# A four-layer graph network: one flat list of steps for layer 3, and its first distances moved into layer 2

## The chip, the cores and the metric

The kernel runs on one core of one Trainium2 chip. The metric is the device time of one execution in microseconds (us). Before the change it is 673.0 us, the median of three runs (672.6 to 673.97).

A core has engines that run side by side, each with its own queue of instructions, which it takes strictly in the written order: TensorE (PE; PEld is its loading of weights), VectorE (DVE), ScalarE (ACT), GpSimd (POOL) and SyncE (SP, which here issues the loads). An instruction that waits holds up everything behind it on its engine.

## The reference, cut to what matters

Four layers share one weighted adjacency matrix of 3327 x 3327 and node features of width 64. Each has the form

```python
h = jnp.maximum(_layernorm(x, axis=-1), 0.0)
x = x + layer(h, adj, ...)
```

Layer 0 is a pair of gated graph convolutions, layer 1 a sum over neighbours in hyperbolic space, layer 2 a sum over the last 100 neighbours of each node with halving weights. Layer 3 is attention in hyperbolic space:

```python
x_tan = _logmap0(x, C)
left = x_tan @ att_W[:D] + att_b
right = x_tan @ att_W[D:]
adj_att = jax.nn.sigmoid(left + right.T) * adj
x_local = _logmap(x[:, None, :], x[None, :, :], C)
support_t = jnp.einsum('ij,ijd->id', adj_att, x_local)
return _proj(_expmap(x, support_t, C), C)
```

So for every pair of nodes layer 3 needs a distance (a dot product and a function of it), an attention weight and their product, and then sums over one index.

## The kernel before

The nodes are padded to 26 blocks of 128. Two blocks make one of 13 columns, and the columns form two groups: `GROUPS[0]` (the code's `gs_`) has columns 0 to 5, `GROUPS[1]` (`gf`) columns 6 to 12. The adjacency is streamed from memory in tiles of up to 896 KB. `Stream` issues the loads on SP in the order of use, into a number of slots (four in layer 3), and loads the next tile when `stream.done()` frees one.

**Layer 2.** `count` makes counts of neighbours on PE into one of two PSUM pairs, ACT or DVE turn them into weights (L1676, L1678), and `weigh` sums with these weights on PE (L1690, six matmuls each). `flush` writes out the sums that are still to do. The group `gf` is finished first; its normalization, node terms and first attention terms (`nodes3(gf, ...)`, `early3`) run woven into the counts of `gs_`.

**Layer 3** uses that distances are symmetric. Its work is cut into 13 phases (`PHASES`), each with up to seven column pairs and two halves `b`. Phases 0 to 3 concern columns of `gf` alone, phases 4 to 9 one column of `gs_` each against all of `gf`, phases 10 to 12 columns of `gs_` alone. The steps of a phase, with their engines:

- `distances` (L1223): matmuls into a PSUM pair, in two pieces `i` of four and three columns. `gelus` (L1233, ACT) reads the pair into the tile `sq`; `square` (L1243, ACT) squares it.
- `tanh_d` (L1256) and `tanh_t` (L1280), ACT: attention terms, in the direct and in the turned arrangement; tiles `dir` and `tr`.
- `attention_d` and `attention_t` (L1293, DVE): times the adjacency tile.
- `turned` (L1323, PE): the distances transposed into the PSUM pair 1, in two pieces. `factors_t` (L1330, DVE) multiplies them into `tr`; `factors_d` (L1311, DVE) multiplies `sq` into `dir`.
- `gather_d`, `gather_t` and `singles` (L1339, PE): the sums, in PSUM banks.

The order of all this is written out. `ORDER3` holds three lists: one for phase 0, one that is repeated for phases 1 to 11, one for phase 12. An entry such as `factors_t.1.0.0` means the step of the phase before (late by 1). Three more chains are woven in as generators: `nodes3(gs_, ...)` (node terms of the first group, about 37 pieces), `bound` (a test of the smallest norm, L1584 to L1589) and `finish_f` (the end of `gf`: L1419 to L1447). `weave.tick()` at an entry `tick` moves what is running one piece further; `WAITS3` gives how many ticks pass between pieces. `distances` of phase 4 first completes `nodes3` and runs `bound`.

`nodes3(gs_, ...)` is a serial chain. The sums of layer 2 are evicted to `m_t` (L638 ACT, L640 DVE), turned by PE (L537) and added to `xn` (L997, DVE); mean, centred value `xc`, variance (L1001 to L1024, DVE and ACT, with two loads of ACT tables at L1016 and L989); `h` and `xd` (L1026, L1028, DVE); `xd` turned by PE (L526) and copied to `xs` (L1048); the attention products (L1057, PE); packed rows `rows_i` and `rows_j` (L1116 to L1121); `leftb` (L1139 to L1144). Phases 4 and later need it, phases 0 to 3 don't.

`finish()` (from L1495) ends the kernel: it closes both sums, applies the last maps, and stores. A further block of code for small norms stands behind a branch on `within`, which `values_load` reads into a register, and isn't run with these inputs.

Of the kernel before, what the change touches and what calls it, by code (L numbers as in the profile page):

```python
# [8 lines left out]
F32 = mybir.dt.float32  # L9
# [10 lines left out]
P = 128  # L20
# [132 lines left out]
BETWEEN = len(PHASES)  # L153
PHASES += [Phase((c,), COLS[1]) for c in COLS[0]]
WITHIN = len(PHASES)
# [40 lines left out]
def order3(text):  # L196
    r = []
    for line in text.split("\n"):
        for name, *args in (w.split(".") for w in line.split()):
            r.append((name, *map(int, args)))  # L200
    return r


EARLY3 = ("d0", "t0")
ORDER3 = [
    order3(t)
    for t in (
        """
        distances.0.0.0 gelus.0.0.0 distances.0.0.1 tanh_t.0.1.0 tick.0 tanh_t.0.1.1 tick.0 tick.0
        tick.1 gelus.0.0.1 square.0.0 distances.0.1.0 gelus.0.1.0 tick.0 distances.0.1.1 tick.0  # L210
        tick.0 tick.0 gelus.0.1.1 tick.0 tick.0 square.0.1 tick.1 tick.0 tick.1 tick.1 tick.0
        tick.1 tick.1 distances.-1.0.0 turned.0.0.0 tick.0 tick.0 tanh_d.0.1 tick.0 gelus.-1.0.0
        """,
        """
        factors_t.1.0.0 tick.0 distances.0.0.1 tick.1 turned.1.0.1 attention_d.1.0 tick.1
        tanh_t.0.0.0 singles.2.1 gelus.0.0.1 distances.0.1.0 tick.1 square.0.0 factors_t.1.0.1
        tick.0 turned.1.1.0 factors_d.1.0 gelus.0.1.0 tanh_d.0.0 tick.1 tick.0 gather_t.1.0.0
        attention_t.1.1 end.2 tick.0 distances.0.1.1 gelus.0.1.1 square.0.1 tanh_t.0.0.1 tick.1
        factors_t.1.1.0 singles.1.0 turned.1.1.1 attention_d.1.1 distances.-1.0.0 factors_t.1.1.1
        tanh_d.0.1 tanh_t.0.1.0 tick.0 factors_d.1.1 tick.0 turned.0.0.0 tick.0 attention_t.0.0  # L220
        tanh_t.0.1.1 gather_t.1.1.1 tick.0 gelus.-1.0.0 gather_t.1.1.0 gather_d.1.0 gather_t.1.0.1
        gather_d.1.1
        """,
        """
        distances.0.0.1 factors_t.1.0.0 tick.1 turned.1.0.1 tanh_t.0.0.0 attention_d.1.0 tick.1
        singles.2.1 gelus.0.0.1 distances.0.1.0 square.0.0 factors_t.1.0.1 gelus.0.1.0
        factors_d.1.0 turned.1.1.0 tanh_d.0.0 tick.1 end.2 attention_t.1.1 factors_t.1.1.0
        distances.0.1.1 singles.1.0 attention_d.1.1 gelus.0.1.1 square.0.1 turned.1.1.1
        tanh_t.0.0.1 tick.1 tanh_t.0.1.0 factors_t.1.1.1 gather_t.1.0.1 factors_d.1.1
        gather_t.1.0.0 tanh_d.0.1 gather_d.1.0 gather_t.1.1.0 turned.0.0.0 attention_t.0.0  # L230
        gather_d.1.1 gather_t.1.1.1 factors_t.0.0.0 tanh_t.0.1.1 turned.0.0.1 tick.1
        attention_d.0.0 singles.1.1 tick.1 factors_t.0.0.1 factors_d.0.0 tick.1 tick.1
        turned.0.1.0 end.1 gather_t.0.0.0 tick.1 attention_t.0.1 factors_t.0.1.0 singles.0.0
        turned.0.1.1 attention_d.0.1 factors_t.0.1.1 tick.1 gather_t.0.1.0 factors_d.0.1
        gather_d.0.0 gather_t.0.1.1 gather_t.0.0.1 gather_d.0.1 tick.1 singles.0.1 end.0 tick.1
        """,
    )
]

WAITS3 = (1, 1, 1, 1, 1, 1, 1, 1, 1, 1, 1, 1, 1, 1, 3, 1, 1, 1, 1, 1, 1, 1, 1, 2, 3, 1, 1, 1, 1, 1)


class Stream:
# [67 lines left out]
def gnn_kernel(ctx: ExitStack, tc: tile.TileContext, t, out):  # L313
    nc = tc.nc
    V, S, G, T = nc.vector, nc.scalar, nc.gpsimd, nc.tensor
# [33 lines left out]
    WIDE = 2 * max(g.w for g in GROUPS)  # L349
# [17 lines left out]
    places, _ = places3()  # L367
# [133 lines left out]
    def pair(i):  # L501

        return ps.tile([P, 1024], F32, name="pair", tag=f"pair{i}")

    def bank(i):
        return ps.tile([P, 512], F32, name="bank", tag=f"bank{i}")
# [639 lines left out]


    def wide3(name, tag):
        pool = n3f if tag in EARLY3 else wk
        return pool.tile([P, WIDE], F32, name=name, tag=tag)  # L1150

    STEPS3 = {}
    made3 = set()

    def step3(f):
        STEPS3[f.__name__] = f
# [34 lines left out]
    @step3  # L1191
    def distances(m, b, i):


        nonlocal x2_
        ph = PHASES[m]
        if m == BETWEEN and x2_ is None:
            weave.until(gen_s)
            for _ in bound():
                pass  # L1200
            x2_ = bank(1)
            V.memset(x2_, 0.0)
        lo, hi = chunk(m, i)
        p = pts[m, b, i] = pair(0)
        g, s = ph.g, ph.s
        for c, ts, first in ph.runs:
            a, e = max(lo, first), min(hi, first + len(ts))
            n = (e - a) * P
            if n <= 0:
                continue  # L1210
            ca = ts[a - first]
            j0 = s.off + b * s.w + (c - s.c0) * P
            for rows in (False, True):
                for k in range(2):
                    rs = slice(k * D, (k + 1) * D)
                    i0 = g.off + k * g.w + (ca - g.c0) * P
                    if rows:
                        l, r = rows_j[rs, j0 : j0 + P], rows_i[rs, i0 : i0 + n]
                    else:
                        l = (xs if k == b else xw)[rs, c * P : (c + 1) * P]  # L1220
                        r = xs[rs, ca * P : ca * P + n]
                    o = k * 512 + (a - lo) * P
                    T.matmul(p[:, o : o + n], lhsT=l, rhs=r, start=not rows, stop=rows)  # L1223
# [117 lines left out]
    @step3  # L1341
    def gather_d(m, b):
        nonlocal pp_
        if (m, b) == (n_all - 1, 1):
            assert (m, "singles", 0) in made3
            pp_ = flat(big(GROUPS[1], "sq"))[:, : 4 * P].rearrange("p (s i c) -> p s i c", s=2, i=2)
            copied_singles(0, ps_)
        a = columns(dirs[m, b], PHASES[m].n)
        for c, ts, first in PHASES[m].runs:
            for p, o, lo, hi in runs(ts, place):  # L1350
                for k in range(2):
                    add(
                        p[k * D : (k + 1) * D, o : o + (hi - lo) * P],
                        xd[:, 2 * c + b, :],
                        a[:, k, (first + lo) * P : (first + hi) * P],
                    )
# [236 lines left out]
        yield  # L1593

    n_all = len(PHASES)
    def have(m):
        return 0 <= m < n_all

    @step3
    def end(m):  # L1600

        nonlocal final
        for d in (sqs, dirs, trs):
            for b in range(2):
                d.pop((m, b))
        if m == WITHIN - 1:
            final = weave.add(finish_f())

    def early3():

        for name, *args in (("tanh_t", 0, 0), ("tanh_t", 0, 1), ("tanh_d", 0)):
            made3.add((0, name, *args))
            yield from STEPS3[name](0, *args)


    with ExitStack() as c2:
# [101 lines left out]
        for n in range(len(work)):  # L1718
# [37 lines left out]
            V.tensor_scalar(onesl, last[:12, :].to_broadcast([12, P]), 9.0, None, op0=OP.is_ge)  # L1756
            gen_n = weave.add(nodes3(gf, m_f))
            weave.add(early3(), 1, gen_n)
        flush(len(work) + LAG, len(todo))
        while weave.running:  # L1760
            weave.tick()
        for name, *args in (("attention_t", 0), ("attention_d", 0)):
            made3.add((0, name, *args))
            STEPS3[name](0, *args)
        x0, x1 = bank(2), bank(3)
        for a in (x0, x1):
            V.memset(a, 0.0)
        m_s = evicted(gs_, acc2[0], b_l2)
    c012.close()
    stream.close(range(SLOTS3, SLOTS2))  # L1770


    turn["banks"] = (1,)
    gen_s = weave.add(nodes3(gs_, m_s), waits=WAITS3)

    with ExitStack() as cf:
        wk = cf.enter_context(right("wkf"))

        ps_, x2_, late_, ds_, pp_ = bank(0), None, None, None, None
        V.memset(ps_, 0.0)

        within = n3.tile([1, 1], I32, name="within")
        final = None
        begin, loop, rest = ORDER3
        orders = [(0, begin)] + [(m, loop) for m in range(1, n_all - 1)] + [(n_all - 1, rest)]
        for m, order in orders:
            for name, late_by, *args in order:  # L1790
                if name == "tick":

                    if late_by or m < BETWEEN:
                        weave.tick()
                elif have(m - late_by) and (m - late_by, name, *args) not in made3:
                    made3.add((m - late_by, name, *args))
                    for _ in STEPS3[name](m - late_by, *args) or ():
                        pass
            if m == WITHIN + 1:
                ok = nc.values_load(within, min_val=0, max_val=1)  # L1800
        weave.until(final)
        finish()
    c3.close()


    with ExitStack() as cg:
        cg.enter_context(tc.If(ok < 1))
        g3 = cg.enter_context(right("g3"))
        sums = g3.tile([P, NB, D + 1], F32, name="sums")

# [366 lines left out]
```

## Time and profile before

| What | Value |
|---|---|
| Median of three runs | 673.0 us |
| The profiled execution's own time | 672.22 us |
| Its span, first to last instruction | 670.4 us |
| Mean granted clock of TensorE | 0.977 |
| PE busy, share of the span | 615.3 us, 92% |
| DVE busy | 456.5 us, 68% |
| ACT busy | 389.3 us, 58% |
| First matmul of layer 3 (L1223) | 416.23 us |
| Last matmul of its main part (`singles` 12.1) | 650.33 us |

Times in the text count from the start of the span. The page has the span in 40 equal slices of 16.8 us, with a digit for the busy share in tenths (9 is 90% or more) and a line `PEclk` for the clock granted to TensorE, in tenths of full speed. A row of the waits reads: waiting line, releasing line, us in total, number of times, longest. A row of the timeline reads: start, us, engine and line, operation, tiles with shapes, number of instructions, and in brackets the idle time before it with its releaser. Matmuls overlap, so the time of a group is best read from its start to the start of the next.

### The profile page before, as it was taken

The numbers are of one execution on the slowest core, as the hardware profiler recorded it, in microseconds if no ns is written. First come the engines' busy times: TensorE is split into PE (matmuls) and PEld (weight loads), VectorE is DVE, ScalarE is ACT, GpSimd is POOL, SyncE is SP. The second block draws the span as 40 slices with busy tenths as digits, with TensorE's granted clock in tenths as the row PEclk, the third lists the DMA queues.
The fourth block names the chain that finished last, engine by engine and source line by source line (L and its number), as shares of the span: only waits on it lengthen the run. The fifth ranks groups of instructions, "written<-read, shape, count | busy, mean of one in ns | idle before, by whom it ended". The sixth has DMA issues, their size and how long they took to land.

```text
span 670.4 us, 13972 instructions
## 1 busy us (share of the span) xinstructions
PE 615.3 (92%) x5968; PEld 341.3 (51%) x5968; DVE 456.5 (68%) x725; ACT 389.3 (58%) x561; POOL 9.3 (1%) x19
## 2 busy tenths in 40 slices
PE   2988999999989999899998999599999999999994
PEld 1442334244333334256665666266666666666781
DVE  3231865444688822678648755679999999999876
ACT  3011300220264403298888688879999999999813
POOL 0000000000000000100000100000000000000000
PEclk9999999999999999999999999589999999999997
DMA  8999999179996999998788993226776666666401
GB/s 335 414 388 421 374 374 351 80 258 421 418 415 228 406 417 415 419 376 318 254 272 294 308 332 118 82 62 188 248 228 221 221 221 221 220 197 221 152 2 56
DMA packets 32534, 183.46 MB, mean 274 GB/s; under 512 B 3696, under 2 KB 4752, under 8 KB 32464
## 3 DMA queue, kind: packets, MB, share of 16 engines
q1 hardware_dynamic: 32112, 181.63, 73.7%
q0 software_dynamic: 352, 0.85, 0.5%
q8 instruction: 49, 0.80, 0.5%
q14 instruction: 21, 0.17, 0.1%
HBM read 180.76 MB, written 0.85 MB: 271 GB/s over the span
## 4 chain that ended last, share of the span: by engine, by line
PE 61%; DVE 18%; DMA 9%; ACT 9%; issue 3%; SPq 0%; ACTq 0%; DVEq 0%
PE bank L651 22%; PE bank L1339 11%; DMA adj<-in_adj 8%; PE pair L1666 7%; PE bank L1690 6%; PE pair L1223 4%; DVE dir L1293 2%; DVE dir L1311 2%; PE pair L752 2%; DVE tr L1330 2%; DVE tr L1293 2%; PE pair L1323 2%; ACT w L1678 2%; ACT tr L1280 1%; DVE edges L379 1%
## 5 line engine op out<-in xcount | busy, mean ns | idle before, releaser
L651 PE MATMUL bank<-adj,m_a 128*64 128x384 f32 (+1 forms) x832 | 154.4, 518 | 8.7 <-DMA adj<-in_adj 6.1
L651 PEld LDWEIGHTS bank<-adj,m_a 128*64 128x64 f32 x832 | 56.9, 137 | 96.2 <-issue 70.9
L1678 ACT ACTIVATE w<-pair,ebias 128x896 uint16<-128x896 f32 (+1 forms) x101 | 93.4, 954 | 17.2 <-PE pair L1666 16.0
L651 PE MATMUL bank<-adj,m_b 128*64 128x384 f32 (+1 forms) x416 | 76.9, 515 | 1.9 <-ACT hm L740 1.4
L379 DVE SCALAR_TENSOR_TENSOR edges<-adj,edges 128x1792 bf16<-128x1792 f32 (+1 forms) x24 | 45.0, 1890 | 32.8 <-DMA adj<-in_adj 32.7
L1280 ACT ACTIVATE tr<-leftb,righth 128x256 f32<-128x256 f32 x156 | 66.3, 495 | 0.1
L1635 DVE TENSOR_SCALAR mask<-adj 128x1792 bf16<-128x1792 f32 (+1 forms) x52 | 52.8, 1035 | 18.8 <-PE pair L1666 18.8
L740 ACT ACTIVATE hm<-bank 64x384 f32<-64x384 f32 (+1 forms) x8 | 4.1, 513 | 94.9 <-DVE mh L739 94.6
L1223 PE MATMUL pair<-xs 64*128 64x512 f32 (+3 forms) x120 | 56.3, 556 | 3.1 <-ACT sq L1233 3.1
L1223 PE MATMUL pair<-xs,xw 64*128 64x512 f32 (+3 forms) x120 | 56.3, 556 | 1.2 <-ACT sq L1233 1.1
L1330 DVE SCALAR_TENSOR_TENSOR tr<-pair,tr 128x1024 f32<-128x1024 f32 (+3 forms) x52 | 49.7, 956 | 9.9 <-PE pair L1323 7.5
L1690 PE MATMUL bank<-w,m_b 128*64 128x384 bf16 (+1 forms) x416 | 56.2, 339 | 0.0
L1233 ACT ACTIVATE sq<-pair 128x1024 f32<-128x1024 f32 (+1 forms) x52 | 47.2, 907 | 13.4 <-PE pair L1223 12.7
L651 PEld LDWEIGHTS bank<-adj,m_b 128*64 128x64 f32 x416 | 28.9, 137 | 46.5 <-issue 41.7
L1311 DVE SCALAR_TENSOR_TENSOR dir<-sq,dir 128x1792 f32<-128x1792 f32 (+2 forms) x27 | 52.5, 1946 | 0.0
L1293 DVE SCALAR_TENSOR_TENSOR dir<-dir,adj 128x1792 f32<-128x1792 f32 x26 | 52.4, 2016 | 0.0
L1256 ACT ACTIVATE dir<-leftb,righth 128x1792 f32<-128x1792 f32 (+6 forms) x38 | 48.5, 1307 | 0.0
L1243 ACT ACTIVATE sq<-sq,hg 128x1792 f32<-128x1792 f32 x26 | 46.5, 1790 | 0.8
L1293 DVE SCALAR_TENSOR_TENSOR tr<-tr,adj 128x1280 f32<-128x1280 f32 (+2 forms) x26 | 45.5, 1751 | 0.0
L1339 PE MATMUL bank<-dir,xd 128*64 128x384 f32 (+3 forms) x264 | 43.7, 461 | 0.0
L1339 PE MATMUL bank<-dir,p2c 128*32 128x256 f32 (+1 forms) x424 | 42.7, 345 | 0.0
L1339 PE MATMUL bank<-tr,xd 128*64 128x128 f32 x624 | 42.0, 277 | 0.0
(312 smaller groups left out, 924.3 us busy)
## 6 DMA issues: line engine op xcount, KB each, us to landing
adj<-in_adj SPq DMA_DIRECT2D x108, 896.0 KB, 6.5
adj<-in_adj SPq DMA_DIRECT2D x92, 768.0 KB, 8.3
adj<-in_adj SPq DMA_DIRECT2D x12, 640.0 KB, 4.1
xn<-in_x SPq DMA_DIRECT2D x3, 192.0 KB, 5.2
out<-w SPq DMA_DIRECT2D x3, 192.0 KB, 2.5
xw<-xs POOLq DMA_DIRECT2D x4, 128.0 KB, 4.0
w_l<-in_w_l SPq DMA_DIRECT2D x1, 460.0 KB, 9.7
xn<-in_x SPq DMA_DIRECT2D x1, 256.0 KB, 6.9
```

What stands on the lines that cost most here:

```text
L379: V.scalar_tensor_tensor(e, a, 0.0, e, op0=OP.not_equal, op1=OP.add)
L651: T.matmul(acc[q][h * D : (h + 1) * D, : hi - lo], lhsT=m[:, k, :], rhs=a[:, h * g.w + lo : h * g.w + hi], start=first, stop=last,)
L1223: T.matmul(p[:, o : o + n], lhsT=l, rhs=r, start=not rows, stop=rows)
L1256: S.activation(columns(dirs[m, b], ph.n)[:, :, first * P : first * P + n], left_of(ph.g)[:, :, o : o + n], AF.Tanh, bias=righth[:, 2 * c + ...
L1280: S.activation(a[:, 8 * u * P : (8 * u + 2 * n) * P].rearrange("p (r x c) -> p x r c", r=2, c=D)[:, 2 * i : 2 * i + 2], left_of(ph.s)[:, : ...
L1293: V.scalar_tensor_tensor(a[:, :w], a[:, :w], 1.0, stream.tile(stream.now), op0=OP.add, op1=OP.mult)
L1311: V.scalar_tensor_tensor(a[:, :, cs], s[:, :, cs], HD, a[:, :, cs], op0=OP.add, op1=OP.mult)
L1330: V.scalar_tensor_tensor(a, p, HD, a, op0=OP.add, op1=OP.mult)
L1339: T.matmul(out, lhsT=lhsT, rhs=rhs, start=False, stop=True, skip_group_check=True)
L1635: V.tensor_scalar(masks[n][:, :w], a, 0.0, None, op0=OP.not_equal)
L1678: S.activation(w, e, AF.Relu, bias=ebias)
L1690: T.matmul(acc2[i][q][h * D : (h + 1) * D, : hi - lo], lhsT=p[:, 2 * c + a, :], rhs=ws[n][:, h * g.w + lo : h * g.w + hi].bitcast(BF16), s ...
```

## The change

1. `ORDER3` becomes one flat list that names every step with its own phase number. The pieces of the three woven chains stand in it as `s` (`nodes3(gs_, ...)`), `b` (`bound`) and `f` (`finish_f`). `z` clears the bank `x2_`, and `ok` loads the register of `within`. `WAITS3` and the ticks of layer 3 go.
2. The distances of phase 0, half 0, are issued before the last three calls of `weigh` in layer 2. In phase 0 the second piece uses PSUM pair 1 instead of pair 0.
3. The GELUs of these distances come before the eviction of `m_s`; the three banks of sums are cleared after the eviction, where two were cleared before it.
4. Ten tiles of layer 3 are allocated at the start, in the order of `PLACES3`, in place of allocation at first use.

The core of the diff (the list is cut):

```diff
+PLACES3 = ("d1", "d2", "d3", "s2", "s3", "t2", "t3", "t1", "s0", "s1")
+ORDER3 = order3(
+    """
+    square.0.0 tanh_t.0.1.0 s s s s s s s s tanh_d.0.1 s distances.0.1.0 distances.0.1.1
+    tanh_d.1.0 gelus.0.1.0 gelus.0.1.1 tanh_t.1.0.0 s tanh_t.0.1.1 square.0.1 s s s
+    factors_d.0.0 s s s distances.1.0.0 gelus.1.0.0 s s turned.0.0.0 distances.1.0.1
+    factors_t.0.0.0 turned.0.0.1 tanh_t.1.1.0 gather_t.0.0.0 attention_t.0.1 s s gelus.1.0.1
+    distances.1.1.0 tanh_t.1.0.1 square.1.0 s tanh_t.1.1.1 gelus.1.1.0 s s factors_t.0.0.1
+    turned.0.1.0 attention_d.0.1 distances.1.1.1 gelus.1.1.1 factors_t.0.1.0 s singles.0.0 s
+    s distances.2.0.0 factors_d.0.1 tanh_d.1.1 turned.0.1.1 s s s square.1.1 gather_d.0.0
+    gather_d.0.1 factors_t.0.1.1 gelus.2.0.0 gather_t.0.0.1 gather_t.0.1.0 tanh_t.2.0.0
+    gather_t.0.1.1 distances.2.0.1 turned.1.0.0 singles.0.1 attention_t.1.0 attention_d.1.0
+    tanh_d.2.0 attention_t.1.1 s s factors_t.1.0.0 turned.1.0.1 gelus.2.0.1 factors_d.1.0
+    distances.2.1.0 tanh_t.2.1.0 tanh_t.2.1.1 s s gather_t.1.0.0 tanh_t.2.0.1 tanh_d.2.1
...
+    singles.8.1 gelus.10.1.1 ok distances.11.0.0 tanh_t.10.0.1 square.10.0 turned.9.1.1
...
+    turned.11.1.0 tanh_d.11.1 attention_t.11.1 distances.12.1.0 singles.11.0
+    factors_t.11.1.0 gelus.12.1.0 distances.12.1.1 turned.11.1.1 tanh_t.12.0.1
+    attention_d.11.1 gather_d.11.0 f f f f factors_t.11.1.1 attention_t.12.0 square.12.0
+    gelus.12.1.1 square.12.1 factors_d.11.1 turned.12.0.0 factors_t.12.0.0 gather_t.11.0.1
+    gather_t.11.1.0 gather_d.11.1 gather_t.11.1.1 turned.12.0.1 gather_t.12.0.0 tanh_d.12.0
+    gather_t.11.0.0 attention_d.12.0 factors_t.12.0.1 gather_t.12.0.1 tanh_t.12.1.0
+    tanh_t.12.1.1 attention_t.12.1 turned.12.1.0 factors_d.12.0 singles.11.1 singles.12.0
+    factors_t.12.1.0 turned.12.1.1 gather_d.12.0 tanh_d.12.1 attention_d.12.1
+    factors_t.12.1.1 gather_t.12.1.1 gather_t.12.1.0 factors_d.12.1 gather_d.12.1
+    singles.12.1 s b f
+    """
+)
...
     def distances(m, b, i):
-        nonlocal x2_
         ph = PHASES[m]
-        if m == BETWEEN and x2_ is None:
-            weave.until(gen_s)
-            for _ in bound():
-                pass
-            x2_ = bank(1)
-            V.memset(x2_, 0.0)
         lo, hi = chunk(m, i)
-        p = pts[m, b, i] = pair(0)
+        p = pts[m, b, i] = pair(i if m == 0 else 0)
...
-        flush(len(work) + LAG, len(todo))
...
-        for name, *args in (("attention_t", 0), ("attention_d", 0)):
-            made3.add((0, name, *args))
-            STEPS3[name](0, *args)
-        x0, x1 = bank(2), bank(3)
-        for a in (x0, x1):
-            V.memset(a, 0.0)
-        m_s = evicted(gs_, acc2[0], b_l2)
+        flush(len(work) + LAG, len(todo) - 3)
+        begin3("distances", 0, 0)
+        begin3("distances", 0, 1)
+        flush(len(work) + LAG, len(todo))
+        begin3("attention_t", 0)
+        begin3("attention_d", 0)
...
-    gen_s = weave.add(nodes3(gs_, m_s), waits=WAITS3)
...
-        ps_, x2_, late_, ds_, pp_ = bank(0), None, None, None, None
-        V.memset(ps_, 0.0)
-
+        for tag in PLACES3:
+            places_[tag] = wk.tile([P, WIDE], F32, name=tag[0], tag=tag)
+        begin3("gelus", 0, 0)
+        begin3("gelus", 0, 1)
+        m_s = evicted(gs_, acc2[0], b_l2)
+        x0, x1, ps_ = bank(2), bank(3), bank(0)
+        x2_, late_, ds_, pp_ = None, None, None, None
+        for a in (x0, x1, ps_):
+            V.memset(a, 0.0)
...
+        chains3 = {"s": nodes3(gs_, m_s), "b": bound(), "f": finish_f()}
+        for name, *args in ORDER3:
+            if name in chains3:
+                next(chains3[name], None)
+            else:
+                made3.add((name, *args))
+                for _ in STEPS3[name](*args) or ():
+                    pass
```

## The prediction

> **What bounds the kernel now.** I read the slices of the page first (where each engine has room), then the stretches of layer 3, TensorE's waits on both sides of 443.7 us, and last the timeline of ScalarE (ACT) and VectorE (DVE) in the gap. The slices, then the stretches (columns: PE, PEld, DVE, ACT, POOL busy us with instructions, granted clock, DMA share, GB/s):
>
> ```profile
> PE   2988999999989999899998999599999999999994
> DVE  3231865444688822678648755679999999999876
> ACT  3011300220264403298888688879999999999813
> PEclk9999999999999999999999999589999999999997
> ```
>
> ```profile
> 416.20:443.70 27.50, 18.30 (x98) 9.90 (x96) 18.64 (x49) 19.70 (x28) 2.06 (x4) 0.63 0.25 72
> 443.70:462.10 18.40, 17.93 (x244) 11.43 (x244) 17.31 (x23) 18.00 (x24) 0.00 (x0) 1.00 0.44 129
> 462.10:522.00 59.90, 58.20 (x826) 38.59 (x824) 57.30 (x44) 58.25 (x81) 0.00 (x0) 1.00 0.71 226
> 522.00:604.50 82.50, 81.15 (x1216) 54.56 (x1216) 79.46 (x51) 79.23 (x112) 0.00 (x0) 1.00 0.68 221
> 604.50:650.30 45.80, 44.90 (x657) 32.87 (x657) 40.03 (x35) 30.76 (x44) 0.00 (x0) 1.00 0.40 129
> ```
>
> After 443.7 us three engines are nearly full and PE is the fullest: its idle time there is 0.47 + 1.70 + 1.35 + 0.90 = 4.4 us in 206.6. Before that, layer 3 starts with a hole: PE works 18.3 of 27.5 us, at a clock of 0.63. So there are two stores to draw on, the hole and 4.4 us. TensorE's waits, first 416.2 to 443.7, then 462.1 to 650.3:
>
> ```profile
> PE bank L526 <- DVE xd L1028: 4.4, 1, 4.4
> PE pair L1223 <- ACT sq L1233: 2.5, 3, 1.2
> PE bank L526 <- DVE xs L1048: 0.8, 1, 0.8
> ```
>
> ```profile
> PE pair L1223 <- ACT sq L1233: 1.7, 2, 0.9
> PE pair L1323 <- DVE tr L1330: 1.6, 6, 0.3
> PE bank L1589 <- DVE low L1586: 0.4, 1, 0.4
> ```
>
> The hole is the node chain of the first group (`nodes3(gs_)`, a serial run over DVE, ACT and PE): PE stands 4.4 us for `xd`. ACT and DVE in the hole:
>
> ```profile
> 424.45 1.02 ACT L1233 ACTIVATE sq<-pair 128x1024 f32<-128x1024 f32 x1 [1.26 <-PE pair L1223]
> 425.37 0.83 ACT L1005 ACTIVATE sq<-xc 128x768 f32<-128x768 f32 x1
> 427.10 1.28 ACT L1016 ACT_TABLE_LOAD   x1
> 440.15 1.02 ACT L1233 ACTIVATE sq<-pair 128x1024 f32<-128x1024 f32 x1 [5.46 <-PE pair L1223]
> ...
> 419.36 0.54 DVE L640 TENSOR_SCALAR m_t<-bank,w_all 128x384 f32<-128x384 f32 x1
> 430.84 0.96 DVE L1028 TENSOR_TENSOR xd<-h,f_th 128x768 f32<-128x768 f32 x1
> ```
>
> `xc` is ready at 424.4, but its square waits behind a GELU until 425.37; later ACT stands 5.46 us for a distance.
>
> **What the Trainium skill says.** "Trainium Architecture — The Big Picture", Inside one NeuronCore: each engine has its own instruction stream, and the streams meet only at semaphores. So the order of a list matters through what stands ahead in an engine's own queue; the 0.95 us of the square agree. "TensorE: Matmul & The Clock Gate", What's actually happening: half clock after an idle window of about 3.4 us, full clock after one of sustained work, the window running freely. The trace agrees in size: the clock falls at about 421.9 and returns at about 442.0, 7 us after PE's work became dense at 434.96. "ScalarE: Activation LUTs", What ACT_TABLE_LOAD costs: 1283 ns, and about 1380 ns more for a drain. The load of 1.28 us agrees; the drain doesn't show (the previous activation ends at 427.08), so I use 1.28.
>
> **The change, part by part.** No arithmetic is added or removed. The sum is made against the profiled execution (span 670.4, own time 672.22, so 1.8 us lie around it); the median of the runs is 673.0, 0.8 more, and I subtract the gain from that. Step times are starts to next starts: distances of four columns 1.2 us, of three 1.0; GELU 0.92 and 0.72; square 1.70; one tanh of `tr` 0.40, `dir` 1.7 to 1.9; `factors_d` and `attention_d` 1.94, `attention_t` 1.4 to 1.95, `factors_t` 1.15, 0.87 or 0.35; a whole `gather_d` 1.55, `gather_t` 0.95, `singles` 1.65.
>
> *Distances ahead of the last three weighted sums.* They use both pairs and need the last ReLUs: ACT ends at 414.06, DVE at 414.99. They issue at 414.65 instead of 416.23, and the three groups of sums (3 x 0.49) end near 418.4 instead of 416.1. Queued behind them are the two evictions `m_t`. DVE's start came at 419.36 before, after two attentions and two memsets; now the memsets follow it, so it runs at 418.4, and the three memsets (0.48 each) hold the first add until 420.35, against 420.65. That is 0.3 us. ACT finishes both GELUs by 417.9, and evicts its half at 418.6. The late sums cost nothing under this cover; without it they would cost 1.5 to 2.3.
>
> *The node chain.* In the flat list ACT has only a square and four tanh ahead of it (free at 422.3), so `xc` squares at 424.2 instead of 425.37. With the two table loads and DVE's sequence unchanged, `xd` ends at 430.55 instead of 431.80: 1.25 us. The rest keeps that lead: the attention products (2.7 us at half clock) end at 436.45, not 437.68, and distances 1.0.0 issue at 436.4, not 437.61.
>
> *Work pulled into the hole.* While PE waits, ACT also does `tanh_d` 1.0 and a `tanh_t`, DVE `factors_d` 0.0. That gives ACT and DVE a store of some 3 us, but only what PE gains shortens the end. Up to 443.75 PE still waits 0.35 us twice (for a GELU, and for DVE's packs behind `attention_t` 0.1). From there it has, in list order up to distances 2.1.0: distances 5.7 (1.2, 1.05, 1.2, 1.05, 1.2), turned blocks 1.8, packs and `leftb` 1.8, `singles` 3.3, gathers 4.5, in all 17.1 us. Walking the releasers by hand with these durations, I find each ready when PE comes to it. So these distances end at 460.8 instead of 462.2: lead **1.4 us**. Clock: if it returns late, at 442.0 as before, about 0.6 is lost; if early, at 438.6, nothing; below nothing is excluded by this walk, which has the early one.
>
> *The remaining phases.* In a loop phase PE's own work is 16.2 of 16.49 us (81.15 of 82.5 in five), DVE's 16.1, ACT's 15.8. No order beats 16.2. The list can recover only the 3.95 us of idle time after 462.1, against waits of its own. With a store of 3 us on DVE and ACT, a hand walk through phases 5 to 7 finds one wait of 0.15 us. I take three quarters: **3.0 us**; the ends are all of it plus waits shorter than the modelled matmul ends (0.3 a phase, 13 phases: 8), and below nothing, minus 4, if the list waits twice as much as the loop did.
>
> *The tail.* From distances 12.1.1 PE has 22.5 us left, while DVE's 18.0 plus the last half gather, `picked` and `singles` (3.0) make 21.0: PE still ends last, and `finish` after it (20.1 us) is unchanged. Nothing gained.
>
> *Small edits.* Memset of `x2_` as a step, 0.5 us on DVE, in its store. The register load of `within`, on all five queues, moves from after phase 11's loop to phase 10: before, no engine shows a gap for it, so 0 (up to 0.3). On SP it now stands ahead of five tile loads, but its value was written some 90 us earlier; the order of the attentions, and so of the loads, is unchanged: 0. The preallocated places make first writes wait on old readers, all done by 414: 0.
>
> Sum: 1.4 + 3.0 = 4.4; 673.0 - 4.4 = **668.6 us**.
>
> **The rivals.** *A: lead only.* The list waits as often as the loop; gain 1.4 (1.0 to 2.0), 671.6. For: the queues have less regular order. Against: the stores. *B: more than visible.* The list removes the short waits hidden under the modelled ends; 8 us, 665. For: identical PE groups differ by 0.1 to 0.2 us. Against: PE's gaps don't show it. *C: slower, ACT holds pair 0.* All distances after phase 0 go through one PSUM pair, which only a GELU frees; the flat list puts tanh runs (up to seven, 2.8 us) and squares ahead of GELUs. 48 distances remain; at 0.15 us each that is 7.2 us, less 4.4: +2.8, 675.8. It decides from 4.4 / 48 = 0.09 us per distance. For: already 1.7 us of PE's waits are this one, and my walk has margins of 0.05 us in places. Against: ACT has 0.6 us of room a phase. *D: it does nothing for the end*, the chain's lead being lost to the half clock: 672.8.
>
> **How the numbers follow.** Forecast 0.53 (its own range 666.5 to 670.8), A 0.17, B 0.12, C 0.11, D 0.07. A measurement can tell 0.2%, 1.3 us, from no change. A splits, 0.12 faster and 0.05 the same: faster 0.53 + 0.12 + 0.12 = 0.77, same 0.05 + 0.07 = 0.12, slower 0.11. The range takes in A, D and most of B: 664.0 to 673.5, leaving out C and a little of B.
>
> **What would show it.** Right: `xd` of the first group ends 1 to 1.5 us earlier; its square follows `xc` at once; PE's idle time after the hole under 2.5 us; the last `singles` before 647. Wrong: the wait of distances on GELUs above 4 us in sum (C), DVE's `factors_t` waiting on turned blocks as much as before (A), or the clock still at half after 443 (D).

## The result, and the profile after the change

| | Before | After |
|---|---|---|
| Median of 20 runs each | 673.49 us | 670.01 us |
| Ratio of the runs, 95% interval | | 0.9938 (0.992 to 0.9956) |
| The profiled execution, its span | 672.22, 670.4 us | 670.23, 668.2 us |
| Mean granted clock | 0.977 | 0.974 |

The change makes the kernel 0.62% (0.44% to 0.8%) faster, 4.2 us by the ratio and 3.5 us by the medians. The forecast was 4.4 us less, and 668.6 us as a time; of the 1.4 us between that and 670.01, 0.5 us lie in the starting value (673.0 was the median of three runs, 673.49 is that of twenty).

The slices of the page of after:

```profile
PE   1987999999989999899998999599999999999994
DVE  3230866444588821677657755789999999999875
ACT  3111300120263503198888788889999899999823
PEclk9999999999999999999999999779999999999896
```

The slices are nearly those of before. The clock's dip in the hole reads 77 in place of 58. A new digit stands near the end: 8 in the third slice from the right, from about 618 us on, with PE at 9. I come back to it.

In this execution the earlier layers took 0.89 us longer: the last matmul of the counts starts at 414.23 us, before at 413.34. The same stretches, shifted by 0.89 us, the last one up to its end at 647.8 (columns as in the prediction: span, PE, PEld, DVE, ACT, POOL, clock, DMA share, GB/s):

```profile
417.09:444.59 27.50, 18.52 (x122) 11.38 (x118) 21.59 (x50) 23.59 (x35) 2.06 (x4) 0.69 0.27 74
444.59:462.99 18.40, 17.45 (x235) 11.06 (x235) 17.52 (x23) 16.46 (x25) 0.00 (x0) 1.00 0.63 205
462.99:522.89 59.90, 59.90 (x873) 39.71 (x871) 56.68 (x44) 57.02 (x75) 0.00 (x0) 1.00 0.64 215
522.89:605.39 82.50, 81.43 (x1198) 54.34 (x1194) 78.26 (x51) 76.89 (x109) 0.00 (x0) 1.00 0.65 214
605.39:647.80 42.41, 42.41 (x629) 31.71 (x624) 37.72 (x33) 29.96 (x45) 0.00 (x0) 0.96 0.40 132
```

In the hole ACT now works 23.6 us (19.7 before) and DVE 21.6 (18.6): work was pulled into it. From 463 us on PE's idle time is 0 + 1.07 + 0 us, before 1.70 + 1.35 + 0.90. The last stretch is 3.4 us shorter, though its clock is 0.96. TensorE's waits in the hole, three of the lines:

```profile
PE bank L577 <- DVE xd L1079: 5.4, 1, 5.4
...
PE bank L577 <- DVE xs L1099: 0.8, 1, 0.8
...
PE pair L1270 <- ACT s L1280: 0.3, 1, 0.3
```

And from 463 to 647.8 us, all there is:

```profile
PE pair L1270 <- ACT sq L1280: 1.1, 1, 1.1
```

The six waits for `tr` and the wait of `bound` are gone. The timeline of ACT and DVE in the hole:

```profile
425.05 0.84 ACT L1056 ACTIVATE sq<-xc 128x768 f32<-128x768 f32 x1 [1.76 <-DVE xc L1054]
...
433.64 1.69 ACT L1280 ACTIVATE s<-pair 128x1024 f32<-128x1024 f32 x2
...
419.13 0.61 DVE L691 TENSOR_SCALAR m_t<-bank,w_all 128x384 f32<-128x384 f32 x1
419.85 1.57 DVE L1842 MEMSET bank<- 128x512 f32 x3
421.32 0.67 DVE L1048 TENSOR_TENSOR xn<-xn,bank 128x512 f32<-128x512 f32 x1
...
424.06 0.96 DVE L1054 SCALAR_TENSOR_TENSOR xc<-ln_mean,xn 128x768 f32<-128x768 f32 x1
...
430.52 0.96 DVE L1079 TENSOR_TENSOR xd<-h,f_th 128x768 f32<-128x768 f32 x1
```

The square of `xc` starts as `xc` ends (424.06 + 0.96 us); ACT waited for it, not it for ACT. The GELUs of distances 0.1, of which the first stood ahead of that square before, come at 433.64, after the table loads.

**One measure for all kernels.** A single execution scatters by some 3 us, much of it outside the change: the last count matmul, behind identical layers 0 to 2, starts between 412.24 and 415.80 us in the traces here. So I split layer 3 of each trace at the last packed-row matmul of distances 2.1.0: the *lead part* runs to it from the last count matmul, the *order part* from it to the first matmul of `finish`. The dip is what the clock costs near 620 us: half of 3.4 us at half clock, an estimate (the order parts of after and `late`, with the same list, differ by 1.57 us).

```text
kernel        lead part  order part  dip   order less dip   ratio (95%)
before          48.50      188.49     -       188.5         1
after           47.05      186.54    1.7      184.8         0.9938 (0.9920 to 0.9956)
b_ahead         48.31      190.09    1.7      188.4         0.9992 (0.9973 to 1.0011)
late            46.95      184.97     -       185.0         0.9932 (0.9909 to 0.9955)
head            46.35      188.44     -       188.4         0.9994 (0.9972 to 1.0016)
tail            47.53      186.05     -       186.1         0.9982 (0.9965 to 0.9998)
slow_chain      50.13      186.51    1.7      184.8         0.9985 (0.9969 to 1.0002)
mend            46.62      184.65     -       184.7         0.9929 (0.9907 to 0.9952)
warm            46.79      186.58    1.7      184.9         0.9925 (0.9893 to 0.9958)
mend_warm       46.33      184.65     -       184.7         0.9930 (0.9904 to 0.9956)
mend_spread     46.81      184.73     -       184.7         0.9915 (0.9888 to 0.9941)
mend_warm8      45.65      184.65     -       184.7         0.9909 (0.9882 to 0.9936)
best            45.41      184.73     -       184.7         0.9926 (0.9899 to 0.9954)
```

Ratios are against runs of the kernel before in the same session. The order part of one list repeats within 0.2 us, less the dip. The lead part doesn't: with one and the same list it is 47.05 us in after, 46.74 in `low_work` (below) and 46.35 in `head`, where the clock came back to full 28.5, 28.0 and 27.2 us after the last count matmul. The ratio can't tell 0.2% from nothing.

### The profile page after: what moved, and what is told of

Its sections match the earlier page's. It is cut to its first block, busy times and chain, and to the rows that moved or that the text cites. A ratio compares the mean times of both kernels' runs of the same rounds, so it can differ in the third digit from the quotient of the medians.

```text
span 668.2 us, 13997 instructions
## 1 busy us (share of the span) xinstructions
PE 614.5 (92%) x5968; PEld 341.9 (51%) x5968; DVE 455.6 (68%) x725; ACT 387.2 (58%) x561; POOL 9.3 (1%) x19
## 4 chain that ended last, share of the span: by engine, by line
PE 72%; DVE 10%; DMA 9%; ACT 7%; issue 2%; SPq 0%; DVEq 0%; ACTq 0%
PE bank L702 22%; PE bank L1386 17%; DMA adj<-in_adj 8%; PE pair L1270 8%; PE pair L1715 7%; PE bank L1739 6%; PE pair L1370 3%; PE pair L803 2%; ACT w L1727 2%; DVE edges L430 1%; PE bank L1483 1%; PE pair L607 1%; DMA xn<-in_x 1%; ACT tr L1327 1%; PE bank L577 1%
## 5 line engine op out<-in xcount | busy, mean ns | idle before, releaser
L1727 ACT ACTIVATE w<-pair,ebias 128x896 uint16<-128x896 f32 (+1 forms) x101 | 93.3, 953 | 17.2 <-PE pair L1715 16.1
L1327 ACT ACTIVATE tr<-leftb,righth 128x256 f32<-128x256 f32 x141 | 59.9, 500 | 3.0 <-PE bank L1386 3.0
L1377 DVE SCALAR_TENSOR_TENSOR tr<-pair,tr 128x1024 f32<-128x1024 f32 (+3 forms) x46 | 44.7, 971 | 9.1 <-PE pair L1370 8.5
L1340 DVE SCALAR_TENSOR_TENSOR dir<-dir,adj 128x1792 f32<-128x1792 f32 x23 | 46.4, 2016 | 0.0
L1280 ACT ACTIVATE sq<-pair 128x1024 f32<-128x1024 f32 (+1 forms) x44 | 39.9, 908 | 9.8 <-PE pair L1270 6.6
L1358 DVE SCALAR_TENSOR_TENSOR dir<-sq,dir 128x1792 f32<-128x1792 f32 (+2 forms) x23 | 44.4, 1934 | 0.0
L1303 ACT ACTIVATE dir<-leftb,righth 128x1792 f32<-128x1792 f32 (+6 forms) x32 | 42.7, 1362 | 0.1
L1340 DVE SCALAR_TENSOR_TENSOR tr<-tr,adj 128x1792 f32<-128x1792 f32 (+2 forms) x23 | 41.0, 1785 | 0.6 <-ACT tr L1327 0.5
L1290 ACT ACTIVATE sq<-sq,hg 128x1792 f32<-128x1792 f32 x22 | 39.1, 1782 | 0.1
L1739 PE MATMUL bank<-w,h_t 128*64 128x384 bf16 x208 | 37.9, 339 | 0.0
L1715 PE MATMUL pair<-mask,rest_a 128*64 128x384 bf16 x192 | 33.5, 342 | 4.5 <-ACT w L1727 4.4
## 6 DMA issues: line engine op xcount, KB each, us to landing
w_l<-in_w_l SPq DMA_DIRECT2D x1, 460.0 KB, 10.1
```

Source lines behind the costliest of these rows:

```text
L1327: S.activation(a[:, 8 * u * P : (8 * u + 2 * n) * P].rearrange("p (r x c) -> p x r c", r=2, c=D)[:, 2 * i : 2 * i + 2], left_of(ph.s)[:, : ...
L1340: V.scalar_tensor_tensor(a[:, :w], a[:, :w], 1.0, stream.tile(stream.now), op0=OP.add, op1=OP.mult)
L1358: V.scalar_tensor_tensor(a[:, :, cs], s[:, :, cs], HD, a[:, :, cs], op0=OP.add, op1=OP.mult)
L1377: V.scalar_tensor_tensor(a, p, HD, a, op0=OP.add, op1=OP.mult)
L1715: T.matmul(cnt[h][s * D : (s + 1) * D, P + lo : P + hi], lhsT=l, rhs=r, start=first and j == 0, stop=j == len(terms) - 1 or first and s == ...
L1727: S.activation(w, e, AF.Relu, bias=ebias)
```

## The experiments

My theory: 1.4 us come from the node chain's lead, 3 us from the later order; the early distances only fill the wait for the last weighted sums. The rivals: the early distances bring the gain; or it is all in one of the two other parts. Lines in these kernels are one or two lower than in after.

**The early distances alone** (`b_ahead`): the new code with the old order written out as a flat list.

```diff
-    square.0.0 tanh_t.0.1.0 s s s s s s s s tanh_d.0.1 s distances.0.1.0 distances.0.1.1
+    tanh_t.0.1.0 s tanh_t.0.1.1 s s s square.0.0 distances.0.1.0 gelus.0.1.0 s distances.0.1.1
...
```

> The old order of steps, written as a flat list, with only the early distances, the memsets behind the eviction and the tiles allocated at the start. Theory (the lead comes from what stands ahead of the node chain in ACT's queue and from work pulled into the hole, the rest from fewer TensorE waits): the square of xc still waits behind a GELU, so only about 0.3 to 0.8 us are gained; the stretch from the last counts of layer 2 to the end of the last singles, 237.0 us before and 233.6 after, is 236.4 here, ratio 0.999. Rival (the early distances bring the gain): stretch 233.6 to 234.5, ratio 0.994.

Measured: 672.14 us, ratio 0.9992. The first add comes 0.2 us earlier after the last count matmul, the lead part is 0.19 us shorter, less than the 0.3 us expected, the order part the old one. PE's waits are those of before (1.7, 1.6 and 0.4 us). The flat list as such and the early distances bring nothing that can be measured.

**Everything but the early distances** (`late`):

```diff
-        flush(len(work) + LAG, len(todo) - 3)
+        flush(len(work) + LAG, len(todo))
         begin3("distances", 0, 0)
         begin3("distances", 0, 1)
-        flush(len(work) + LAG, len(todo))
```

> The changed kernel with the distances of phase 0 behind all weighted sums again; the flat list is kept. Theory: DVE's attentions hide most of the late sums; the node chain starts about 0.3 us later or not at all, so the stretch is 233.6 to 234.2 us, ratio 0.994 to 0.996. Rival (the early distances bring the gain): stretch 236.5, ratio about 1.0.

Measured: 668.63 us, ratio 0.9932, no slower than after. Their place shows in the chain (`xd` ends 17.55 us after the last count matmul, in after 17.25), not in the time.

**The list cut in two at distances 2.1.0.** `head` has the new order up to there, then the old one; `tail` the reverse.

```diff
@@ head
     distances.2.1.0
-    tanh_t.2.1.0 tanh_t.2.1.1 s s gather_t.1.0.0 tanh_t.2.0.1 tanh_d.2.1
+    s square.2.0 factors_t.1.0.1 s turned.1.1.0 gelus.2.1.0 s s gather_t.1.0.0
...
```

> The changed kernel with the new order only up to the distances 2.1.0, and the old order from there. Theory: the lead of 1.4 us stays and the old order's waits come back: stretch 235.0 to 235.8 us, ratio 0.997 to 0.998. Rival one (all gain is in the head of the list): 233.6, ratio 0.994. Rival two (the lead is eaten later): 237, ratio 1.0.

> The changed kernel with the old order up to the distances 2.1.0, and the new order from there. Theory: no lead from the node chain, but the fewer waits of the rest: stretch 234.5 to 235.5 us, ratio 0.995 to 0.997. Rival one (all gain is in the head): 236.5 to 237, ratio 1.0. Rival two (all gain is in the rest of the list): 233.6, ratio 0.994.

PE's waits of `head` from 462 us on, and then those of `tail`:

```profile
PE pair L1268 <- ACT sq L1278: 1.7, 2, 0.9
PE pair L1368 <- DVE tr L1375: 1.6, 6, 0.3
PE bank L1634 <- DVE low L1631: 0.4, 1, 0.4
```

```profile
PE bank L1188 <- ACT leftb L1191: 1.9, 1, 1.9
PE pair L1268 <- ACT sq L1278: 1.1, 1, 1.1
```

`head` keeps the lead and has all the old waits; `tail` has lost them, with one larger wait for `leftb` where the two orders meet. In the traces each half shows its part: 2.2 us of lead in `head`, 2.4 us of order in `tail`. But both traces had luck with the clock, as TensorE was at full clock in distances 0.1.0: `head` has 0.7 us more of lead than after with the same list, and `tail` has 1.0 us of lead with the old one, as its GELU was out of the way of `xc`. In the times the parts are smaller, 0.06% and 0.18% against 0.62% for both, so both ratios miss the expected ranges. The missing 0.38% (0.05 to 0.71%, the intervals taken as independent) is just outside the noise and isn't explained; by the medians of the same runs, 1.15 and 2.05 us under before, the parts come near the 3.5 us of after. So the traces tell where the gain lies, and the times only that neither half alone brings it all.

**Does a lead of the chain reach the end?** `slow_chain` computes `xd` of the first group four times, to the same place.

```diff
-        V.tensor_mul(xd[:, sl, :], h[:, sl, :], bc(qv))
+        for _ in range(4 if g is gs_ else 1):
+            V.tensor_mul(xd[:, sl, :], h[:, sl, :], bc(qv))
```

> The changed kernel with the product xd of the node chain computed four times in place of once (same values), three extra DVE products of 0.96 us: the chain of nodes is 2.9 us longer, nothing else changes. Theory (a lead of the chain reaches the end of layer 3 nearly whole, since PE has no other work in the hole and none to spare after it): turned distances, attention products and all later work start 2.9 us later, and the time rises by 2.0 to 2.9 us over that of the changed kernel, to a ratio of 0.997 to 0.998. Rival (the lead is absorbed, as the engines have work stored up after the hole, and the gain comes from the later order alone): less than 1 us, ratio 0.994 to 0.995.

DVE's group, and PE's wait for it (5.4 us in after):

```profile
431.82 3.94 DVE L1078 TENSOR_TENSOR xd<-h,f_th 128x768 f32<-128x768 f32 x4
```

```profile
PE bank L575 <- DVE xd L1078: 8.7, 1, 8.7
```

Measured: 672.32 us, ratio 0.9985 against 0.9938: 3.2 us more (1.5 to 4.8, the two intervals taken as independent); 2.0 to 2.9 was expected. The lead part grew by 3.08 us, for 2.97 us of extra products, and the order part by nothing (186.51 and 186.54). So a delay of the chain is passed on whole, and the rival, a lead that is absorbed, is out. That every further lead is gained whole doesn't follow: in `mend_warm8` below, 1.9 us of it leave 1.0.

**Two waits that my walk had missed** (`mend`). The memsets hold the first add by 0.5 us; and at 455.80 us ACT stands 1.6 us, because `tanh_t` 2.0.0 writes the tile that a `gather_t` of phase 0 still reads, after which PE stands 0.8 us for `leftb`.

```diff
-        for a in (x0, x1, ps_):
-            V.memset(a, 0.0)
...
+    def clear(i):
+        V.memset((x0, x1, ps_)[i], 0.0)
...
-    factors_d.0.0 s s s distances.1.0.0
+    factors_d.0.0 clear.0 clear.1 clear.2 s s s distances.1.0.0
...
-    tanh_t.2.0.0 gather_t.0.1.1
+    tanh_d.2.0 tanh_t.2.0.0 gather_t.0.1.1
...
-    tanh_d.2.0 attention_t.1.1
+    attention_t.1.1
```

> The changed kernel with two things moved in its list: the three memsets of the banks of sums stand behind factors_d of phase 0 in place of ahead of the node chain's first add, and tanh_d 2.0 stands ahead of tanh_t 2.0.0. Theory: the first add starts 0.5 us earlier (0.6 us behind PE's transposed sums instead of behind three memsets of 0.52 us), and the chain with it; ACT no longer stands 1.6 us for the gather that reads the old tile of tanh_t, so PE's 0.8 us wait for leftb goes; sum 0.8 to 1.3 us, time 668.7 to 669.3, ratio 0.992 to 0.9926. Rival: another wait is late next and the time stays within 0.4 us of the changed kernel's.

The waits of ACT from 443 us to 461.1 us, first line:

```profile
ACT tr L1325 <- DVE t L1375: 0.9, 1, 0.9
```

The first add starts 0.56 us earlier, distances 1.0.0 0.33 us. ACT's wait became one for `factors_t`, 0.9 us, and PE's wait for `leftb` 0.5 us. In the trace that is 0.43 us of lead and 0.2 us of order. The 0.2 us stand: the order part is 184.65 to 184.73 us in all five kernels with these moves, and 184.8 to 185.0 less the dip without them. The 0.43 us are not shown to come from the moves: `low_work`, with the list of after and the clock back 28.0 us after the last count matmul as in `mend`, has a lead part of 46.74 us, `mend` 46.62. The ratio, 0.9929, can't be told from after's. Both theory and rival got half: another wait was late next.

**The half clock on the chain.** `warm` repeats the matmuls of distances 0.1.1 in PE's idle time, four times in all; `mend_warm` adds the moves of `mend`; `mend_warm8` repeats them eight times.

```diff
+        again = 4 if (m, b, i) == (0, 1, 1) else 1
-        for c, ts, first in ph.runs:
+        for c, ts, first in ph.runs * again:
```

> The changed kernel with the matmuls of distances 0.1.1 done four times into the same PSUM tile (same result): three extra groups of 1.0 us at full clock, 2.0 at half, in PE's idle 5.4 us ahead of the transposes of xd. Theory (the half clock on the node chain is a consequence of PE's idle time, and costs what the slow groups lose): the clock stays up or returns by 431, the attention products take 1.4 instead of 2.7 us, distances 1.0.0 1.2 instead of 2.3, and layer 3 ends 1 to 2.5 us earlier, ratio 0.990 to 0.9925. Rival one: at half clock the extra work lasts to 432 and holds the transposes of xd, the time rises by up to 1 us. Rival two: the groups at half clock are covered by ACT and DVE, who set the pace there, and nothing changes, ratio 0.994.

> Both at once: the moved memsets and the moved tanh_d 2.0, and the matmuls of distances 0.1.1 done four times. Theory: the sums add, 1.8 to 3.5 us less than the changed kernel, 666.5 to 668.2, ratio 0.9890 to 0.9915. Rival: the warm clock makes PE wait for ACT instead, and no more is gained than by the moves alone, 668.7 to 669.3.

> The moved memsets and tanh_d 2.0, with the matmuls of distances 0.1.1 done eight times in place of four: PE's idle time ahead of the transposes of xd shrinks from 3.3 to 4.9 us to some 1.7. With four times the clock came to full during the repeats and fell again about when xd's transposes began, so the attention products still took 2.7 us. Theory: now it stays full, the attention products take 1.4 us, distances 1.0.0 1.2 instead of 2.3 us, and layer 3 ends 1 to 2 us earlier than with the moves alone: 666.5 to 668, ratio 0.990 to 0.992. Rival: ACT and DVE set the pace of the first phases (their tanh and GELU steps are due then anyway), and the time stays at 668.5 to 669.5, ratio 0.9925 to 0.994; or the repeats at half clock hold the transposes, +1 us.

PE at the transposes of `xd` and the attention products, in `warm` and then in `mend_warm8`:

```profile
432.82 0.84 PE L575 MATMUL bank<-ident,xd 128*128 128x128 f32 x4 [3.29 <-DVE xd L1077]
434.44 0.69 PE L575 MATMUL bank<-ident,xd 128*128 128x128 f32 x2 [0.79 <-DVE xs L1097]
435.64 2.72 PE L1106 MATMUL bank<-w_all,xs 128*128 128x4 f32 x12 [0.52 <-DVE xs L1097]
```

```profile
429.92 0.63 PE L575 MATMUL bank<-ident,xd 128*128 128x128 f32 x4 [1.63 <-DVE xd L1077]
431.33 0.44 PE L575 MATMUL bank<-ident,xd 128*128 128x128 f32 x2 [0.79 <-DVE xs L1097]
432.29 1.50 PE L1106 MATMUL bank<-w_all,xs 128*128 128x4 f32 x12 [0.52 <-DVE xs L1097]
```

The clock came up at 426.3 us in `warm`, but so it does without repeats in after (425.7). With four repeats it stayed up until 433.1 us, in after until 429.1; 3.3 us of that were idle, and the products took 2.72 us as in after. So the expectation for `warm` failed in its mechanism, although its ratio lies at the edge of the range. With eight, in `mend_warm8`, they took 1.50 us, but the next distances were at half clock again (1.04 us a group). And in `best` below, with the same eight repeats, the clock fell just before the products, at 434.9 us, and they took 2.72 us: that eight repeats keep it up is not shown. Distances 1.0.0 of `mend_warm8` came 1.9 us earlier than in `mend`, the lead part shrank by only 1.0 us; PE then waited 0.9 us for an ACT square. Ratios: 0.9925, 0.9930 and 0.9909. `mend_warm` came out as its rival had it, no better than the moves alone; the time of `mend_warm8` is in the range of its theory, but its interval overlaps that of `mend`.

**The dip near 620 us.** Granted clock (third value from the right) in after, before, at and past the first two-column matmuls of `finish_f` (`halves`):

```profile
616.00:618.00 2.00, 2.00 (x24) 1.27 (x20) 2.00 (x2) 2.00 (x7) 0.00 (x0) 1.00 0.81 287
618.00:620.10 2.10, 2.10 (x26) 2.06 (x26) 2.10 (x3) 2.10 (x6) 0.00 (x0) 1.00 0.23 40
620.10:623.50 3.40, 3.40 (x50) 2.50 (x44) 2.38 (x2) 2.07 (x3) 0.00 (x0) 0.52 0.71 258
623.50:625.50 2.00, 2.00 (x34) 1.12 (x34) 1.63 (x2) 0.50 (x1) 0.00 (x0) 0.96 0.91 246
```

PE counts as busy all through, and yet the clock is at half for 3.4 us. Four of the first ten traces show this (the expectation below says eleven; I had miscounted): `after`, `b_ahead`, `slow_chain`, `warm`. In each of them the dip begins 0.1 to 0.4 us after a run of these matmuls has ended. `low_work` does these matmuls three times each:

```diff
-            for i in range(lo, hi):
+            for i in [*range(lo, hi)] * (3 if g is gf else 1):
```

> The changed kernel with the two-column matmuls of finish_f (the tiles named halves) done three times each into the same places (same result): PE gets 2 x 28 such matmuls more, the first run of them in one go of 5.7 us instead of 1.9. In the trace of the changed kernel TensorE's clock is at half for 3.4 us right after them, though PE counts as busy all along; four of eleven traces here show this. Theory (matmuls of two columns count as idle time for the clock): here the clock surely falls during or after them, for 3.4 us or 6.8, and the time rises by the extra matmuls (3.8 + 2.8 us) and 1.7 to 3.4 us for the clock, 8.3 to 10 us in all, ratio near 1.007. Rival (the dips have nothing to do with them and fall at chance): the clock stays full after them as in most traces, the time rises by 6.6 us or less, ratio 1.003 or below.

The same four stretches in `low_work`:

```profile
614.30:616.30 2.00, 2.00 (x24) 1.27 (x20) 2.00 (x2) 2.00 (x7) 0.00 (x0) 1.00 0.75 276
616.30:618.40 2.10, 2.10 (x22) 2.08 (x19) 2.10 (x3) 2.10 (x6) 0.00 (x0) 0.98 0.28 51
618.40:628.30 9.90, 9.90 (x73) 8.80 (x74) 2.37 (x2) 2.06 (x3) 0.00 (x0) 0.50 0.47 152
628.30:630.30 2.00, 2.00 (x34) 1.12 (x36) 1.32 (x2) 0.19 (x1) 0.00 (x0) 0.94 0.00 0
```

Half clock for some 10 us with PE full, and a second dip of 3.4 us at the end of the second run of them, at 639 us. Time 680.09 us, ratio 1.0097: 10.1 us over after by the medians, 10.7 by the ratios (8.1 to 13.3), where the theory said 8.3 to 10 and the rival at most 6.6. So a longer run of these matmuls brings the clock down. That the short dips have the same cause is argued from where they begin, and not shown: six of the first ten traces have none after the same matmuls. `mend_spread` moves one of their two pieces apart:

```diff
-    factors_d.11.0 f f singles.10.1
+    factors_d.11.0 f singles.10.1
...
-    distances.12.1.0 singles.11.0
+    distances.12.1.0 f singles.11.0
```

> The kernel with moved memsets and moved tanh_d 2.0 (669 us), and the second piece of finish_f with two-column matmuls moved behind distances 12.1.0, some 4 us later, so that only 0.95 us of them stand in a row instead of 1.9. Theory: the dip of TensorE's clock after them becomes rarer; it came in three of seven executions of this order at about 1.7 us each, so the mean falls by up to 0.7 us, to 667.8 to 668.5, ratio 0.9915 to 0.993, and this trace shows no dip there. Rival: PE's move of 0.95 us makes another step late, same time as without it or up to 1 us more.

Measured: 667.59 us, 0.9915, no dip and no new wait in the trace. But `mend` had none either, and the two ratios overlap. That spreading makes the dip rarer is not shown; in `b_ahead` it came after a single piece of 0.94 us.

**All at once** (`best`):

> All that helped at once: the moved memsets and tanh_d 2.0, the second piece with two-column matmuls moved behind distances 12.1.0, and the matmuls of distances 0.1.1 done eight times. Theory: the gains add, as they lie in different places (the first add, the attention products, the clock near 620 us): 3.0 to 4.0 us less than the changed kernel, 666 to 667 us, ratio 0.989 to 0.991. Rival: the parts that seemed to add 0.5 to 1 us each were scatter between runs, and the time is that of the moves alone, 667.8 to 668.6, ratio 0.992 to 0.993.

Measured: 668.21 us, 0.9926. By its trace it is the shortest (45.41 + 184.73 us), by its time it isn't: the rival's number came out. The five kernels with the moves lie between 0.9909 and 0.9930, after at 0.9938, and no interval parts any of them from it. A better version than after is suggested by the trace (1.8 us less than after without its dip), but 1.6 us of that are lead, which goes with the clock, and the times don't show it.

## Why the prediction held, step by step

- **Early distances.** Forecast and measured, the latter less the 0.89 us: issue at 414.65 and 414.77, last sums over at 418.4 and 418.5, DVE's `m_t` at 418.4 and 418.2, first add at 420.35 and 420.43. `b_ahead` and `late` show them worth 0.2 to 0.3 us in the chain, as said.
- **The node chain.** `xd` ends at 430.59 (forecast 430.55), the attention products at 436.53 (436.45), distances 1.0.0 issue at 436.47 (436.4). The square no longer waits for a GELU: that is 0.95 of the 1.21 us, and `late`, without the early distances, has `xd` 0.9 us earlier than before. The rest is mainly the earlier first add.
- **Lead.** Distances 2.1.0 end at 460.77 (460.8), so the 1.4 us came, but in part by luck: two errors cancel. The walk had the clock back at 438.6; it came back at 441.9 (442.75 in the trace), the late case, for which I had set 0.6 us of loss. The third value from the right is the clock:

```profile
442.00:442.70 0.70, 0.70 (x6) 0.34 (x6) 0.70 (x1) 0.52 (x2) 0.00 (x0) 0.50 0.00 0
442.80:443.50 0.70, 0.70 (x16) 0.63 (x14) 0.70 (x4) 0.49 (x1) 0.00 (x0) 1.00 0.00 0
```

  Against that, only one of the two waits of 0.35 us came, of 0.3 us; PE reached the distances 1.1.0 at 443.70, forecast 443.75. `slow_chain` shows a delay of the chain passed on one to one. The walk missed one wait just after its end: PE's 0.8 us for `leftb`, behind ACT's 1.6 us on a tile that was still being read. I had asked of each step what data it needs, not who still reads the tile that it writes. The clock was as much of a risk as said: in `head` it was up in distances 0.1.0 and back sooner, and the lead part was 0.7 us shorter still. That the clock before "agrees in size" with a window of 3.4 us was generous: the 7 us that it took to return are about two of them.
- **Remaining phases.** Forecast 3.0 of 3.95 us. Stretches of the same work, from the end of distances 2.1.0 on, in before and then in `late`, which has the list of after and no dip:

```profile
462.22:650.33 188.11, 184.17 (x2693) 125.96 (x2692) 176.68 (x128) 168.24 (x234) 0.00 (x0) 1.00 0.62 200
```

```profile
461.97:646.56 184.59, 182.69 (x2691) 125.02 (x2692) 173.95 (x127) 165.22 (x230) 0.00 (x0) 1.00 0.60 197
```

  The stretch is 3.5 us shorter. Idle time gave 3.94 - 1.90 = 2.0 us of it, less than the 3.0 forecast, because of the 0.8 us for `leftb` and 1.1 us for a GELU. The other 184.17 - 182.69 = 1.5 us is busy time for the same matmuls. I had priced that at nothing: "No order beats 16.2" was wrong. It lies in the `singles` (tile `p2c`), here in before and in `late`, these matmuls alone:

```profile
462.22:650.33 188.11, 41.28 (x984) 33.23 (x984) 0.00 (x0) 0.00 (x0) 1.00 0.62 200
```

```profile
461.97:646.56 184.59, 39.58 (x984) 33.43 (x984) 0.00 (x0) 0.00 (x0) 1.00 0.60 197
```

  They take 1.7 us less (and 41.27 in `head`, with the old order). On PE, six pairs of them stand back to back in `late`, and such a pair takes 2.90 to 3.18 us from its start to the next group's; a single one takes 1.64 to 1.68, as all do in before, where no two are neighbours. Why a pair is cheaper these traces don't say. So this is not rival B's mechanism, short waits spread over all groups and hidden under the modelled ends; it is one that neither I nor a rival had, and it covered the shortfall in the visible part by luck. (DVE's work in a loop phase is 15.9 us by the stretch that the prediction shows, 79.46 in five, and not 16.1; nothing rests on it.)
- **What I left out.** The dip of the clock, 1.7 us, in some executions of either order. With it the traced gain is 1.45 + 1.95 = 3.4 us, without it 5.1 us; the measured 4.2 us (3.0 to 5.4) lies between. So the closeness of 4.2 to 4.4 is partly luck too: with the clock up the order is worth 3.5 us and more, not 3.0, and the dips take some of it back. How often they come in either order isn't known.
- **Tail.** PE has no wait in it, and ACT idles 6.8 us before `finish`: PE-bound as said. `finish` took 20.4 us (20.1 before); the traces range from 19.9 to 21.1.
- **Small edits.** No wait in after or `late` is put down to the memset of `x2_` or the register load. ACT waits 3.0 us in all for `tr` tiles that are still being read, before not at all; whether that comes from the order or from the preallocated places was not tested apart.

Of the signs that I had named, `xd` is 1.21 us earlier, PE's idle time after the hole is 1.9 us, and GELUs hold the distances for 1.1 us, far from rival C's 4. The last `singles` end at 647.8 us, 646.9 less the late start. One sign was badly chosen: DVE's `factors_t` wait for turned blocks as long as before (9.4 us, before 6.9), which I had put down for rival A. It says nothing, since DVE isn't the bound; PE's wait on `factors_t`, 1.6 us before and none after, was the one to name. Rival A falls by the order part, rival D by the lead part and by the clock, which is at full before 443. Rival C falls by PE's waits, rival B by its 8 us: the traces have 5.1 without the dip.

## What to carry to other kernels

Here a serial chain that feeds the bound engine passed a delay on whole (3.1 us), and a lead until another wait came last: look first for foreign work ahead of it in the queues (one GELU, 0.95 us). In a stage where the bound engine is 98% busy, a new order won half of the idle time that the profile shows (2.0 of 3.9 us); and it changed the busy time as well, since like groups of matmuls that stand back to back took 1.7 us less in all. So don't take an engine's busy time for fixed when the order changes. Walk the queues not only for data, but for tiles that are still being read. And compare traces by stretches of the same work: the order parts repeated within 0.2 us here, where whole executions scattered by 3.

## What the hardware showed that I had not expected

- A long run of two-column matmuls didn't keep TensorE's clock up, though the profile counts PE as busy throughout. 1.9 us of them (about one in one trace) were followed by 3.4 us of half clock in four of the thirteen traces other than `low_work`; in `low_work`, with 8.6 us of them in one go, the clock fell after 2 us and stayed down for some 10. The Trainium skill, "TensorE: Matmul & The Clock Gate", What's actually happening, tells of a free-running window of about 3.4 us that watches how busy PE has been. The length of a dip agrees; but if so, busy there is not what the profile calls busy, and a chance overlap with the window would explain why the same list dips in one execution and not in the next. Layer 2 has the like with true idle time: in every trace PE stands 1.96 us near 366 us, and in five of the fourteen the clock falls for 3.4 us during it or within 1.5 us after it. The overlap itself isn't in the trace.
- The attention products, four columns each, may be of the same kind: in `mend_warm8` the clock fell right after them (1.50 us for the products, then 1.04 us instead of 0.69 for the first group of distances), but PE had also been idle for 2.9 of the 5.4 us before, so this trace can't tell the two apart, and it was not tested alone.
